# Second layer's first 1x1 convolution as seven block products, with the sums of h kept in the residual buffer's place

## Chip, cores and metric

The kernel runs on one core of one Trainium2 chip. The metric is the device time of one execution in microseconds; three executions of the kernel before gave 2811.97 to 2815.28, median 2813.42.

## What is computed

Two bottleneck layers in float32, on 64 images of 1024 channels and 14 x 14 positions:

```python
# layer 0: three convolutions with batch norm and a residual
out = relu(bn(conv1x1(x, w1)))            # 1024 -> 256
out = relu(bn(conv3x3(out, w2)))          # 256 -> 256
h   = relu(x + softplus(s) * bn(conv1x1(out, w3)))   # 256 -> 1024
# layer 1: a deformable bottleneck with group norm
a   = relu(group_norm(conv1x1(h, w1b)))   # 1024 -> 256, the convolution that is changed
off, mask = conv3x3(a, w_off)             # 27 offset and mask channels
s   = bilinear_sample(a, offsets) * mask  # 9 taps
b   = relu(group_norm(einsum(s, w2b)))    # 9 x 256 -> 256
out = relu(h + group_norm(conv1x1(b, w3b)))   # 256 -> 1024
```

## The kernel before

Images go in 32 pairs of 392 columns (196 for each image). Layer 0 runs first, in three stages up to about 960 us of the span; batch norm needs all images. Layer 1 is a software pipeline over the pairs. One pass of it is called a **slot** here: slot t runs the sampling and the second convolution of pair t, the first convolution and the offsets of pair t+1, the third convolution of pair t-1, and fetches h of pair t+2. Slots 2 to 29 are written by `steady`, where the order of the instructions on TensorE, VectorE, ScalarE and GpSimd is the order in which the list `todo` is run. The other slots are written by `slot`, where that holds for TensorE alone and a scheduler orders the rest. Every engine, and SyncE's queue of transfers, works its instructions off in order.

`put` and `at` weave work into a list of matmul steps: a step at position k is emitted ahead of the k-th matmul step. `weave` mixes two lists evenly.

A slot goes in this order on TensorE:

1. `first_conv(t+1)`, 16 products of 392 columns (L1130): eight blocks of input channels for each of two blocks of output channels. Each product is two matmul instructions. ScalarE copies a finished bank to `a1` (L1138), VectorE takes its statistics (L1006).
2. `sampling(t, 0)` (L1455) woven with the first half of `third_conv(t-1)` (L1704). Sampling multiplies by S, the product of the row and column weights that `corners` forms on VectorE (L1435, three pieces).
3. The offset convolution (L1226) of pair t+1, which reads X, four combinations of the columns of `a1` that VectorE writes (L1202) after the norm and relu (ScalarE, L1161).
4. `sampling(t, 1)` woven with the rest of the third convolution. The offsets `off` (L1257) and the mask go to DRAM and come back spread over the partitions as `wt` (SyncE, L1284); L1273 takes the largest offset; L1296 adds the base positions.
5. `second_conv(t, 0)` and `second_conv(t, 1)` (L1567), 35 and 28 products of 196 columns. This convolution and the third are done in seven block products for eight: of a 2 x 2 by 2 x 2 block product with blocks a and b, seven products of sums of blocks. The two column blocks are the two images of the pair. VectorE forms the sums of the sampled values in place (L1523); the banks are emptied by additions: E is a copy of the first bank (ScalarE), V is the second bank plus E (VectorE), and GpSimd adds V to E and to the fourth part.

The third convolution does its seven products m = 0 to 6 for each of four blocks of output channels, in the order 0, 2, 1, 3. V is L1711, GpSimd's two additions are L1716, and the two outputs are L1720 and L1724. Its product 6 is added to the bank half that product 3 wrote, after V has read it:

```python
bank = q["bank", 1 if m == 6 else m // 2]
nc.tensor.matmul(bank[:, m % 2 if m < 6 else 1], a, b, start=(m < 6), ...)
```

The banks of the first and third convolution and of the transposes come from one pool of three.

A group norm is a chain on VectorE from L1016 to L1054, a power on GpSimd (L1055), and the scale and shift on VectorE (L1071, L1075, L1078). gn1 belongs to the first convolution, gn2 to the second, gn3 to the third.

h of pair t+2 is made in place: SyncE loads the third convolution of layer 0, ScalarE scales it (L1096), two transfers on GpSimd's queue add x (L1102), ScalarE applies relu (L1111). For pairs up to 3 the sum is made on VectorE with `Z0` as a buffer (L213). From slot 2 on `Z0` is unused, except in a second run of the layer, which only starts if an offset is larger than 2.

`output` adds h to the scaled third convolution (L1803), applies relu (L1805) and stores; `scaled` is the scaling on ScalarE (L1787).

Of the kernel before, what the change touches and what calls it, by code (L numbers as in the profile page):

```python
# [10 lines left out]
FP = mybir.dt.float32  # L11
AF = mybir.ActivationFunctionType
ALU = mybir.AluOpType
# [7 lines left out]
CB = 8  # L21
# [23 lines left out]
def kernel(  # L45
# [823 lines left out]
    make_identity(nc, ident)  # L869


    goff = const.tile([P, MB * T, 32], FP, tag="goff", name="goff")
# [21 lines left out]

    Sb = {n: const.tile([P, 512], FP, tag=f"Sb{n}", name=f"Sb{n}") for n in (1, 2, 4)}
    Sb[3] = a21

    c11, c12, c21, c22 = (w2b_sb[:, c, :, ts(o, P)] for o in range(2) for c in range(2))
    Sc = {n: const.tile([P, T, P], FP, tag=f"Sc{n}", name=f"Sc{n}") for n in (1, 2, 4)}
# [25 lines left out]

    def build_second_bottleneck(l1, path, run, early):
        groups, R, tapsets = path.groups, path.rows, path.tapsets
        QR = R * W
        starts = sorted({r0 for _, _, chunks in groups for r0 in chunks})

# [177 lines left out]
        def first_relu(p):  # L1108
            for b in range(0, CB, 2):
                y = Y[p % 4][:, ds(b, 2)]  # L1110
                nc.scalar.activation(y, y, AF.Relu)  # L1111

        def residual(p, b0=0, b1=CB):

            for b in range(b0, b1):

                tc.keep_in_program_order(end_of_first(p, Z0, b))
                relu_of_first(p, b)

        def first_conv(p, by_inputs=False):  # L1120
            q = pairs[p]

            def step(o, c):
                if o == c == 0:
                    q["a1"] = two.tile([P, MB, N2], FP, tag="a1", name=f"a1_{p}")
                    q["gn1"] = Norm(MB, 8, N1S, N1B, f"gn1_{p}")
                    q["pt"] = {}
                if c == 0:
                    q["pt"][o] = ps.tile([P, N2], FP, tag="ps", name=f"d1_{p}_{o}")
                nc.tensor.matmul(  # L1130
                    q["pt"][o],
                    w1b_sb[:, c, ts(o, P)],
                    q["y"][:, c, :],
                    start=(c == 0),
                    stop=(c == CB - 1),
                )
# [7 lines left out]
            return [lambda o=o, c=c: step(o, c) for o, c in order]  # L1144

        def norm_steps(norm):

# [98 lines left out]
        def offsets(p):  # L1246
            q = pairs[p]
            half = W // 2
            (even, odd), (m0, m3) = q["sums"], (q["po"][ts(m, 32)] for m in (1, 3))

            q["om"] = one.tile([32, N2], FP, tag="off", name=f"off_{p}")
            for h0, h1, _ in groups:
                dst = q["om"][:, cols(h0, h1)].rearrange("p (i q n) -> p i q n", i=2, n=2)
                for n, (a, b, op) in enumerate(((even, m0, ALU.add), (odd, m3, ALU.subtract))):
                    a = a.rearrange("p (i q) -> p i q", i=2)
                    a, b = (v[:, :, h0 * half : h1 * half] for v in (a, b))
                    nc.vector.tensor_tensor(dst[:, :, :, n], a, b, op)  # L1257
# [165 lines left out]
                    .to_broadcast([R, W, piece.stop - piece.start]),  # L1423
                )

        def corners(p, e):

            q = pairs[p]
            S, X = q["S"][e], q["X"][e]
            k0, k1 = tapsets[e]  # L1430
            q["S"][e] = {}
            for g, r0, piece in pieces(e):

                tc.keep_in_program_order(
                    nc.vector.tensor_tensor(S[:, piece], S[:, piece], X(piece), ALU.mult)  # L1435
                )
                q["S"][e][g, r0] = S[:, piece].rearrange("q (k i n) -> q k i n", k=k1 - k0, i=2)

        def sampling(p, e):

            q = pairs[p]
            k0, k1 = tapsets[e]
            kt = k1 - k0
            out = []

            def step(turn, g, h0, h1, chunks, c, i0, ni):
                if turn == 0:
                    q["sm"][e] = sample_buffer(e, f"sm_{p}_{e}").rearrange(
                        "p (c k i q) -> p c k i q", c=MB, i=2, q=HW
                    )  # L1450
                n = (h1 - h0) * W
                pt = ps_s.tile([P, ni, kt, n], FP, tag="ps_s", name=f"sp_{p}_{e}_{g}_{c}_{i0}")
                for i in range(ni):
                    for j, r0 in enumerate(chunks):
                        nc.tensor.matmul(  # L1455
                            pt[:, i],
                            q["aT"][:, i0 + i, c, starts.index(r0), :],
                            q["S"][e][g, r0][:, :, i0 + i, :],
                            start=(j == 0),
                            stop=(j == len(chunks) - 1),  # L1460
                        )
# [300 lines left out]
        def third_norm(p, both=True):  # L1762
            q = pairs[p]

            def end():
                q["gn3"][0].scale(tc.keep_in_program_order)
                for m in range(2 if both else 1):
# [9 lines left out]
        def scaled(p, m):  # L1777

            q = pairs[p]
            n = q["gn3"][0]  # L1780
            if m in q.setdefault("scaled", set()):
                return
            q["scaled"].add(m)
            for b in range(m, CB, 2):
# [67 lines left out]
        def weight_sums():  # L1852
            for n, a, b, op in (
# [5 lines left out]

                tc.keep_in_program_order(nc.vector.tensor_tensor(Sb[n], a, b, op))  # L1860

        def slot(t):


# [31 lines left out]
            if d1:  # L1896
                extra = list(zip((5, 5, 8, 12, 12, 13, 13, 14), norm2)) + [(10, w) for w in weights[:1]]
                extra = sorted(extra + [(6, s) for s in late], key=lambda v: v[0])
                todo = put(d1, [s for _, s in extra], [k for k, _ in extra])
# [58 lines left out]
        def steady(t):  # L1958
# [9 lines left out]
            def at(steps, *extra):  # L1968
# [21 lines left out]
            todo += at(  # L1990
                pd[0],
                ((1, 1, 1, 9), norm3),
                ((5, 20), [lambda e=e: first_sum(t, e) for e in range(2)]),
                ((6, 11, 16, 21), transposes(t + 1)),
                ((6, 13), [distances, end]),
            )
            todo += [lambda: list(spread_rows(t + 1, 0)), lambda: list(spread_columns(t + 1, 0))]
            todo += [lambda: list(spread_rows(t + 1, 1)), lambda: lend(t + 1)]
            todo += at(pd[1], ((0,), [lambda: first_relu(t + 2)]), ((16,), [lambda: output(t - 1, 0)]))
            todo.append(lambda: list(spread_columns(t + 1, 1)))  # L2000
            for step in todo:
                step()
# [200 lines left out]
```

## Time and profile before

| | |
|---|---|
| median of 3 runs | 2813.42 us (2811.97 to 2815.28) |
| the profiled execution's own time | 2814.66 us |
| span of its instructions | 2812.9 us |
| granted TensorE clock | 0.991 |
| busy: TensorE, VectorE, ScalarE, GpSimd | 2750.9, 2264.8, 1424.8, 1043.1 us |
| first convolution of layer 1, L1130 | 1024 instructions, 345.3 us |
| second convolution, L1567 | 2232 and 1674 instructions, 400.6 and 308.3 us |
| transfers | 424.20 MB, mean 151 GB/s |

PE is TensorE, PEld its weight loads, DVE VectorE, ACT ScalarE, POOL GpSimd, SP SyncE. A line of the timeline gives the start in us from the span's start, the duration, engine, line, operation, out<-in, shape, count, and in brackets the idle time of the engine just before and what ended it. A row with a count covers neighbours that were merged. An instruction that does not depend on the one before it on its engine starts a little before that one's end.

### The profile page before, as it was taken

The numbers are of one execution on the slowest core, as the hardware profiler recorded it, in microseconds if no ns is written. First come the engines' busy times: TensorE is split into PE (matmuls) and PEld (weight loads), VectorE is DVE, ScalarE is ACT, GpSimd is POOL, SyncE is SP. The second block draws the span as 40 slices with busy tenths as digits, with TensorE's granted clock in tenths as the row PEclk, the third lists the DMA queues.
The fourth block names the chain that finished last, engine by engine and source line by source line (L and its number), as shares of the span: only waits on it lengthen the run. The fifth ranks groups of instructions, "written<-read, shape, count | busy, mean of one in ns | idle before, by whom it ended". The sixth has DMA issues, their size and how long they took to land.

```text
span 2812.9 us, 39583 instructions
## 1 busy us (share of the span) xinstructions
PE 2750.9 (98%) x12930; PEld 2016.8 (72%) x12930; DVE 2264.8 (81%) x4676; ACT 1424.8 (51%) x2835; POOL 1043.1 (37%) x1125
## 2 busy tenths in 40 slices
PE   9999899998999999999999999999999999999996
PEld 5555555554555567887888788878887888888874
DVE  7877899998888878878777878788778787777776
ACT  0000221212555546666666676667666766676653
POOL 4630366663666312323332333233323332332221
PEclk9999999999999999999999999999999999999998
DMA  8656000003555444667576657665767576657641
GB/s 236 191 172 175 23 1 0 1 1 132 215 197 219 177 137 167 165 169 196 161 168 175 194 154 173 176 190 153 173 173 200 146 175 177 193 147 175 183 125 48
DMA packets 350317, 424.20 MB, mean 151 GB/s; under 512 B 27892, under 2 KB 292500, under 8 KB 349844
## 3 DMA queue, kind: packets, MB, share of 16 engines
q1 hardware_dynamic: 291860, 376.61, 41.3%
q0 software_dynamic: 58240, 44.96, 11.3%
q8 instruction: 104, 1.70, 0.3%
q14 instruction: 113, 0.93, 0.1%
HBM read 296.49 MB, written 116.76 MB: 147 GB/s over the span
## 4 chain that ended last, share of the span: by engine, by line
PE 59%; DVE 2%; issue 1%; DMA 1%; SPq 0%; ACT 0%; POOL 0%; DVEq 0%; ACTq 0%; POOLq 0%
PE pd L1567 21%; PE sp L1455 12%; PE d L1130 11%; PE d L1704 10%; PE om L1226 2%; PE tr L1333 1%; DMA X<-wd 1%; PE pd L1486 1%; DMA wt<-dm 0%; DVE st L1006 0%; SPq L1374 0%; DVE sm L1523 0%; DMA wd<-wt 0%; SPq L1418 0%; DVE z L1818 0%
## 5 line engine op out<-in xcount | busy, mean ns | idle before, releaser
L1455 PE MATMUL sp<-S,aT 126*128 126x420 f32 (+3 forms) x1536 | 487.0, 415 | 8.0 <-DVE S L1435 5.5
L1567 PE MATMUL pd<-sm,w2b_sb 128*128 128x196 f32 x2232 | 400.6, 329 | 0.0
L1463 ACT COPY sm<-sp 128x336 f32<-128x336 f32 (+3 forms) x640 | 282.8, 447 | 187.8 <-PE sp L1455 167.7
L1567 PEld LDWEIGHTS pd<-sm,w2b_sb 128*128 128x128 f32 x2232 | 371.2, 190 | 0.0
L1523 DVE TENSOR_TENSOR sm<-sm 128x980 f32<-128x980 f32 (+2 forms) x257 | 268.5, 1055 | 120.9 <-PE pd L1567 116.8
L530 PE MATMUL c<-v,u_sb 128*128 128x392 f32 x1024 | 342.6, 497 | 11.0 <-DVE bn1sh L167 8.2
L1130 PE MATMUL d<-h,w1b_sb 128*128 128x392 f32 x1024 | 345.3, 495 | 2.7 <-ACT h L224 2.7
L1567 PE MATMUL pd<-sm,Sc 128*128 128x196 f32 x1674 | 308.3, 329 | 0.6 <-DVE sm L1523 0.6
L530 PEld LDWEIGHTS c<-v,u_sb 128*128 128x128 f32 x1024 | 194.6, 191 | 158.9 <-issue 11.3
L1130 PEld LDWEIGHTS d<-h,w1b_sb 128*128 128x128 f32 x1024 | 194.0, 191 | 139.5 <-ACT h L224 6.4
L1567 PEld LDWEIGHTS pd<-sm,Sc 128*128 128x128 f32 x1674 | 278.7, 190 | 1.1 <-ACT wt L1297 0.9
L1455 PEld LDWEIGHTS sp<-S,aT 126*128 126x128 f32 x1536 | 258.5, 191 | 20.7 <-issue 9.0
L1787 ACT ACTIVATE z<-z,gn_0sh,gn_0sc 128x196 f32<-128x196 f32 x496 | 225.1, 536 | 18.0 <-DVE gn_0sh L1078 18.0
L1598 POOL TENSOR_TENSOR E<-V,E 128x196 f32<-128x196 f32 x31 | 18.5, 597 | 516.8 <-DVE V L1597 516.8
L516 DVE TENSOR_TENSOR v<-t 128x392 f32<-128x392 f32 x256 | 192.9, 811 | 0.0
L1704 PE MATMUL d<-h,w3b_sb 128*128 128x196 f32 x744 | 174.0, 329 | 0.8 <-ACT h L1619 0.8
L1704 PEld LDWEIGHTS d<-h,w3b_sb 128*128 128x128 f32 x744 | 133.6, 189 | 51.6 <-issue 19.1
L1435 DVE TENSOR_TENSOR S<-S,X 126x840 f32<-126x840 f32 (+1 forms) x192 | 159.5, 880 | 11.7 <-DMA X<-wd 11.3
L1805 ACT ACTIVATE z<-z 128x784 f32<-128x784 f32 x124 | 105.8, 856 | 105.1 <-DVE z L1803 102.7
L385 PE MATMUL c<-xc,w1a_sb 128*128 128x392 f32 x384 | 149.1, 497 | 5.3 <-DMA xc<-in_x_dram 5.3
L1096 ACT ACTIVATE h<-h,bn3sh,bn3sc 128x392 f32<-128x392 f32 x224 | 149.9, 705 | 0.0
L504 POOL TENSOR_TENSOR t<-wpad 128x784 f32<-128x784 f32 x62 | 95.2, 1536 | 127.2 <-DVE v L516 127.2
(693 smaller groups left out, 5044.3 us busy)
## 6 DMA issues: line engine op xcount, KB each, us to landing
xc<-in_x_dram SPq DMA_DIRECT2D x128, 392.0 KB
h<-o SPq DMA_DIRECT2D x64, 784.0 KB
h<-h SPq DMA_DIRECT2D x64, 784.0 KB
out_dram<-z SPq DMA_DIRECT2D x124, 392.0 KB
h<-in_x_dram POOLq DMA_DIRECT2D x56, 784.0 KB, 12.5
X<-wd SPq DMA_DIRECT2D x64, 413.4 KB
S<-wd SPq DMA_DIRECT2D x64, 413.4 KB
S<-wd SPq DMA_DIRECT2D x64, 330.8 KB
```

Of the source, the lines that this page charges most:

```text
L385: nc.tensor.matmul(acc[m], a, b, start=(j == 0), stop=(j == HB - 1))
L516: nc.vector.tensor_tensor(v[:, u].rearrange("p (i y x) -> p i y x", y=7, x=7), cols[c][:, :, i : i + 13 : 2, :], cols[c][:, :, j : j + 13 ...
L530: nc.tensor.matmul(m[u], u_sb[:, c, u, k % 4, ts(o, P)], vts[k][c][:, u], start=(c == 0), stop=(c == MB - 1),)
L1096: nc.scalar.activation(y, y, AF.Identity, bias=bn3.sh[:, b : b + 1], scale=bn3.sc[:, b : b + 1])
L1130: nc.tensor.matmul(q["pt"][o], w1b_sb[:, c, ts(o, P)], q["y"][:, c, :], start=(c == 0), stop=(c == CB - 1),)
L1435: nc.vector.tensor_tensor(S[:, piece], S[:, piece], X(piece), ALU.mult)
L1455: nc.tensor.matmul(pt[:, i], q["aT"][:, i0 + i, c, starts.index(r0), :], q["S"][e][g, r0][:, :, i0 + i, :], start=(j == 0), stop=(j == len ...
L1463: nc.scalar.copy(dst, pt.rearrange("p i k n -> p k i n"))
L1523: return nc.vector.tensor_tensor(dst, a, b, ALU.subtract)
L1567: nc.tensor.matmul(bank[:, m % 2], a[:, k], b[:, k - k0],  start=(k == 0 and m in (5, 0, 2, 6)), stop=(k == T - 1), skip_group_check=True,)
L1704: nc.tensor.matmul(bank[:, m % 2 if m < 6 else 1], a, b, start=(m < 6), stop=True, skip_group_check=True)
L1787: nc.scalar.activation(z[:, ts(i, HW)], z[:, ts(i, HW)], AF.Identity, bias=n.sh[:, b, i : i + 1], scale=n.sc[:, b, i : i + 1],)
```

## The change

From pair 3 on, the first 1x1 convolution of layer 1 is done in seven block products. The 1024 input channels are two blocks of four times 128, the 256 output channels two blocks, the columns the two images. A product is 4 matmul steps of 196 columns, so 28 steps take the place of 16 of 392.

- The sums of the weights are formed once, in slot 1, on VectorE (`first_weight_sums`): three in a new tile `Sa`, one in place in `w1b_sb`. The offset weights' staging tile `goff` now lies in `Sa`.
- The sums of h, T1[1] to T1[4], are formed for each pair on VectorE by `first_sums` in `Z0`: for pair t+2 in slot t, three ahead of the second half of the second convolution and one at its position 22 of 28.
- The banks are emptied as in the third convolution: E by ScalarE, V and the two outputs by VectorE, two additions by GpSimd. `a1` is complete only at the end; before, its first half was copied after half of the products.
- `off` has no tile of its own any more and lies in `wt`'s.
- Positions: `corners(t, 0)` is cut into its three pieces, at 19 and 24 of the 28 steps and behind them; gn2's scale, relus and sums are at 17 to 19; relu of h moves from the start of the second half of the second convolution to position 24 of the first half, ahead of four of the eight scalings of the third convolution's blocks 0, 2, 4, 6.

```diff
+    Sa = const.tile([P, 3, HB, P], FP, tag="Sa", name="Sa")
+    goff = Sa.rearrange("p n k o -> p (n k o)")[:, : MB * T * 32].rearrange("p (n o) -> p n o", o=32)
...
+    e11, e12, e21, e22 = (w1b_sb[:, ts(c, HB), ts(o, P)] for o in range(2) for c in range(2))
+    Se = {1: Sa[:, 0], 2: Sa[:, 1], 3: e21, 4: Sa[:, 2]}
...
+        def first_sums(p, *ns):
+            q, room = pairs[p], Z0.rearrange("p b n -> p (b n)")
+            T1 = q.setdefault("T1", {})
+            y = q["y"]
+            (b11, b12), (b21, b22) = ([y[:, ts(c, HB), ts(i, HW)] for i in range(2)] for c in range(2))
+            for n in ns:
+                T1[n] = room[:, ts(n - 1, HB * HW)].rearrange("p (b q) -> p b q", b=HB)
+                a, b = ((b12, b11), (b22, T1.get(1)), (b22, b12), (b21, T1.get(2)))[n - 1]
+                tc.keep_in_program_order(nc.vector.tensor_tensor(T1[n], a, b, ALU.subtract))
...
         def first_conv(p, by_inputs=False):
+            if early and p >= 3:
+                return first_conv_of_seven(p)
...
+        def first_conv_of_seven(p):
...
+                a, b = (
+                    (e11, b11),
+                    (Se[1], T1[1]),
+                    (Se[2], T1[2]),
+                    (Se[3], T1[3]),
+                    (e12, b21),
+                    (Se[4], b22),
+                    (e22, T1[4]),
+                )[m]
+                if k == 0 and m in (0, 2, 4):
+                    q["bank", m // 2] = ps.tile([P, 2, HW], FP, tag="ps", name=f"d1_{p}_{m}")
+                bank = q["bank", 1 if m == 6 else m // 2]
+                nc.tensor.matmul(
+                    bank[:, m % 2 if m < 6 else 1],
+                    a[:, k],
+                    b[:, k],
...
+                if m == 1:
+                    q["E"] = one.tile([P, 2, HW], FP, tag="E", name=f"E1_{p}")
+                    nc.scalar.copy(q["E"], bank)
+                elif m == 3:
+                    E = q["E"]
+                    V = q["V"] = one.tile([P, 2, HW], FP, tag="V", name=f"V1_{p}")
+                    nc.vector.tensor_tensor(V, bank, E, ALU.add)
+                    nc.gpsimd.tensor_tensor(E[:, 1], V[:, 0], E[:, 1], ALU.add)
+                    nc.gpsimd.tensor_tensor(a1[:, 1, HW:], V[:, 0], V[:, 1], ALU.add)
+                elif m == 5:
+                    nc.vector.tensor_tensor(
+                        a1[:, 0].rearrange("p (i n) -> p i n", i=2), bank, q["E"], ALU.add
+                    )
+                    q["gn1"].stats(0, a1[:, 0])
+                elif m == 6:
+                    nc.vector.tensor_tensor(a1[:, 1, :HW], bank[:, 1], q["V"][:, 0], ALU.add)
+                    q["gn1"].stats(1, a1[:, 1])
+            return [lambda m=m, k=k: step(m, k) for m in range(7) for k in range(HB)]
...
-            q["om"] = one.tile([32, N2], FP, tag="off", name=f"off_{p}")
+            q["om"] = one.tile([KY, 2, N2], FP, tag="wt", name=f"off_{p}")[:32, 0, :]
...
+            if early and t == 1:
+                todo.append(first_weight_sums)
...
+            if early and t == 1:
+                todo.append(lambda: first_sums(3, 1, 2, 3, 4))
...
         def steady(t):
...
                 ((0,), [lambda: scaled(t - 2, 1)]),
-                ((1, 1, 7, 9, 9, 10, 10, 10), norm2),
-                ((6,), [lambda: output(t - 2, 1)]),
-                ((7,), [lambda: load(t + 2, False)]),
-                ((10,), [lambda: corners(t, 0)]),
+                ((2, 2, 17, 18, 18, 18, 18, 19), norm2),
+                ((12,), [lambda: output(t - 2, 1)]),
+                ((13,), [lambda: load(t + 2, False)]),
+                ((19, 24), [lambda n=n: corners(t, 0, n) for n in range(2)]),
             )
+            todo += [lambda: corners(t, 0, 2)]
             todo += at(weave(sp[0], d3[:half]), ((4, 4, 8, 14, 16, 18, 21), norm1))
...
                 pd[0],
                 ((1, 1, 1, 9), norm3),
+                ((24, 25), [lambda: first_relu(t + 2), lambda: scaled(t - 1, 0, 4, CB)]),
...
-            todo += at(pd[1], ((0,), [lambda: first_relu(t + 2)]), ((16,), [lambda: output(t - 1, 0)]))
+            todo += at(
+                pd[1],
+                ((0, 22), [lambda: first_sums(t + 2, 1, 2, 3), lambda: first_sums(t + 2, 4)]),
+                ((16,), [lambda: output(t - 1, 0)]),
+            )
```

More of the change, by code (lines that the diff above doesn't have):

```diff
@@ L869 @@
     make_identity(nc, ident)
-    goff = const.tile([P, MB * T, 32], FP, tag="goff", name="goff")
+    Sa = const.tile([P, 3, HB, P], FP, tag="Sa", name="Sa")
+    goff = Sa.rearrange("p n k o -> p (n k o)")[:, : MB * T * 32].rearrange("p (n o) -> p n o", o=32)
     woff_sb = const.tile([P, 4, MB * 3, 32], FP, tag="woff", name="woff_sb")
@@ L927, in build_second_bottleneck @@
         groups, R, tapsets = path.groups, path.rows, path.tapsets
+        if not early:
+            nc.sync.dma_start(e21, w1b[: HB * P, ds(P, P)].rearrange("(b p) o -> p b o", p=P))
         QR = R * W
@@ L1144, in first_conv, with step @@
             return [lambda o=o, c=c: step(o, c) for o, c in order]
+        def first_conv_of_seven(p):
+            q = pairs[p]
+            def step(m, k):
+                if m == k == 0:
+                    q["a1"] = two.tile([P, MB, N2], FP, tag="a1", name=f"a1_{p}")
+                    q["gn1"] = Norm(MB, 8, N1S, N1B, f"gn1_{p}")
+                y, T1, a1 = q["y"], q["T1"], q["a1"]
+                (b11, b12), (b21, b22) = (
+                    [y[:, ts(c, HB), ts(i, HW)] for i in range(2)] for c in range(2)
+                )
[15 more added lines that the diff above has]
+                    b[:, k],
+                    start=(k == 0 and m < 6),
+                    stop=(k == HB - 1),
+                    skip_group_check=True,
+                )
+                if k < HB - 1:
+                    return
+                if m == 1:
[10 more added lines that the diff above has]
+                        a1[:, 0].rearrange("p (i n) -> p i n", i=2), bank, q["E"], ALU.add
+                    )
+                    q["gn1"].stats(0, a1[:, 0])
[3 more added lines that the diff above has]
+            return [lambda m=m, k=k: step(m, k) for m in range(7) for k in range(HB)]
@@ L1424, in spread_columns, with corners @@
                 )
-        def corners(p, e):
+        def corners(p, e, *ns):
             q = pairs[p]
@@ L1430, in corners @@
             k0, k1 = tapsets[e]
-            q["S"][e] = {}
-            for g, r0, piece in pieces(e):
+            done = q.setdefault(("corner", e), {})
+            for n, (g, r0, piece) in enumerate(pieces(e)):
+                if ns and n not in ns:
+                    continue
                 tc.keep_in_program_order(
@@ L1436, in corners @@
                 )
-                q["S"][e][g, r0] = S[:, piece].rearrange("q (k i n) -> q k i n", k=k1 - k0, i=2)
+                done[g, r0] = S[:, piece].rearrange("q (k i n) -> q k i n", k=k1 - k0, i=2)
         def sampling(p, e):
@@ L1457, in step @@
                             q["aT"][:, i0 + i, c, starts.index(r0), :],
-                            q["S"][e][g, r0][:, :, i0 + i, :],
+                            q["corner", e][g, r0][:, :, i0 + i, :],
                             start=(j == 0),
@@ L1766, in end @@
                 q["gn3"][0].scale(tc.keep_in_program_order)
-                for m in range(2 if both else 1):
+                if not both:
+                    scaled(p, 0, 0, 4)
+                    return
+                for m in range(2):
                     scaled(p, m)
@@ L1775, in third_norm, with scaled @@
             ]
-        def scaled(p, m):
+        def scaled(p, m, b0=0, b1=CB):
             q = pairs[p]
             n = q["gn3"][0]
[L1781 to L1784, printed above, removed]
+            done = q.setdefault("scaled", set())
+            for b in range(b0 + m, b1, 2):
+                if b in done:
+                    continue
+                done.add(b)
                 z = z_of(p, b)
@@ L1860, in weight_sums, with first_weight_sums @@
                 tc.keep_in_program_order(nc.vector.tensor_tensor(Sb[n], a, b, op))
+        def first_weight_sums():
+            for n, a, b, op in (
+                (1, e21, e22, ALU.add),
+                (2, Se[1], e11, ALU.subtract),
+                (3, e11, e21, ALU.subtract),
+                (4, e12, Se[2], ALU.subtract),
+            ):
+                tc.keep_in_program_order(nc.vector.tensor_tensor(Se[n], a, b, op))
         def slot(t):
@@ L1898, in slot @@
                 extra = sorted(extra + [(6, s) for s in late], key=lambda v: v[0])
-                todo = put(d1, [s for _, s in extra], [k for k, _ in extra])
+                todo = put(d1, [s for _, s in extra], [k * len(d1) // 16 for k, _ in extra])
                 todo += put(weave(sp[0], d3[:half]), norm1, (4, 4, 8, 14, 16, 18, 21))
@@ L1998, in steady @@
             todo += [lambda: list(spread_rows(t + 1, 1)), lambda: lend(t + 1)]
-            todo += at(pd[1], ((0,), [lambda: first_relu(t + 2)]), ((16,), [lambda: output(t - 1, 0)]))
+            todo += at(
+                pd[1],
+                ((0, 22), [lambda: first_sums(t + 2, 1, 2, 3), lambda: first_sums(t + 2, 4)]),
+                ((16,), [lambda: output(t - 1, 0)]),
+            )
             todo.append(lambda: list(spread_columns(t + 1, 1)))
```

## Prediction

> **What bounds the kernel now.** The page comes first: TensorE is busy 98% of the span, every other engine 81% or less. The chain that ended last goes on TensorE through the whole second layer, and its products L1130 open a slot every 56.0 us (at 1546.35 and at 1602.35, 10.53 us each).
>
> ```profile
> PE 2750.9 (98%) x12930; PEld 2016.8 (72%) x12930; DVE 2264.8 (81%) x4676; ACT 1424.8 (51%) x2835; POOL 1043.1 (37%) x1125
> ```
>
> So a slot is TensorE work without a gap, and less of it should be a shorter slot. But the average hides the stage that is changed. I cut one slot (t = 11) at its stages: first the products L1130, last the second half of the second convolution.
>
> ```profile
> core 0: us, PE busy (x) PEld busy (x) DVE busy (x) ACT busy (x) POOL busy (x), PEclk, DMA share, GB/s
> 1602.19:1612.72 10.53, 10.53 (x34) 6.08 (x33) 9.10 (x21) 5.92 (x12) 4.36 (x6) 1.00 0.82 262
> ...
> 1648.90:1658.19 9.29, 9.29 (x58) 9.29 (x58) 5.63 (x7) 5.90 (x10) 0.41 (x1) 1.00 0.58 196
> ```
>
> In the first stage VectorE is busy 9.10 of 10.53 us, hardly less than TensorE, and the change shortens TensorE's share and lengthens VectorE's. Next, VectorE's queue through that stage and just behind it, from the timeline (start, duration, idle before):
>
> ```profile
> 1606.62 1.85 DVE L1803 TENSOR_TENSOR z<-z,h 128x784 f32<-128x784 f32 x2
> ...
> 1610.26 3.14 DVE L1435 TENSOR_TENSOR S<-S,X 126x840 f32<-126x840 f32 x3
> ...
> 1614.05 0.31 DVE L1016 STREAM_TRANSPOSE gn_12R<-st 128x128 f32<-128x128 f32 x1
> ...
> 1616.03 0.17 DVE L1054 TENSOR_SCALAR gn_12B<-gn_12B 128x4 f32<-128x4 f32 x1
> 1616.44 0.57 DVE L1711 TENSOR_TENSOR V<-d,E 128x392 f32<-128x392 f32 x1 [0.25 <-PE d L1704]
> 1617.32 0.55 DVE L1071 SCALAR_TENSOR_TENSOR gn_12sc<-gn_12B,vec 128x4 f32<-128x4 f32 x1 [0.30 <-POOL gn_12B L1055]
> 1617.90 0.53 DVE L1075 SCALAR_TENSOR_TENSOR gn_12sh<-gn_12B,gn_12sc 128x4 f32<-128x4 f32 x1
> ...
> 1618.64 0.57 DVE L1720 TENSOR_TENSOR z<-d,E 128x392 f32<-128x392 f32 x1
> 1619.12 0.35 DVE L1724 TENSOR_TENSOR z<-d,V 128x196 f32<-128x196 f32 x1
> ```
>
> The idle times in brackets are all the room there is. TensorE meets this queue twice in the third convolution: its seventh product of the first column block may overwrite a bank only when V (L1711) has read it, and the third product of the second block needs the bank that L1724 empties.
>
> ```profile
> 1602.19 10.70 PE L1130 MATMUL d<-h,w1b_sb 128*128 128x392 f32 x32
> ...
> 1618.02 0.50 PE L1704 MATMUL d<-T,w3b_sb 128*128 128x196 f32 x2
> ...
> 1620.21 0.50 PE L1704 MATMUL d<-T,Sb 128*128 128x196 f32 x2
> ```
>
> V ends at 1617.01, 1.01 us before its product at 1618.02; L1724 ends at 1619.47, 0.74 us before 1620.21. These two margins decide the case.
>
> **What is removed.** 32 matmul instructions of 392 columns take 10.53 us, 0.329 each. 28 products are 56 instructions of 196 columns; L1567 dispatches ten such in 1.66 us, 0.166 each. 56 x 0.166 = 9.29, so 1.24 us less per slot: 54.76 if nothing else moves. The two ScalarE copies L1138 (0.48 each) become one. A rule speaks against this: the Trainium skill, "TensorE: Matmul & The Clock Gate", section "Back-to-back issue gap", gives streams of weight load and matmul 81 ns each at 128 columns and 131 at 512, far from proportional. An estimate by that page (90 ns at 196 columns, 115 at 392) would make the stage 10.53 x 56/32 x 0.78 = 14.4 us, 3.8 us more per slot. The rows here are proportional, with 2232 weight loads hidden, and I go by them.
>
> **What is added to VectorE.** Evictions: one add of 392 from a bank (0.57, as L1711), another (0.57, as L1720), one of 196 (0.35, as L1724): 1.49 us, in the first stage. Sums of h: four subtractions of 784 at 0.97 (row L1523), 3.6 to 3.9 us, in the last stage. A slot's VectorE time goes from 44.2 to about 49.6 of 54.76: it fits on average, so the place decides. GpSimd gets two adds of 196 (0.60 each, as L1598).
>
> **The sums' place.** VectorE idles before the first sm subtraction and before V of the second convolution:
>
> ```profile
> 1650.43 0.98 DVE L1523 TENSOR_TENSOR sm<-sm 128x784 f32<-128x784 f32 x1 [3.22 <-PE pd L1567]
> ...
> 1657.13 0.57 DVE L1597 TENSOR_TENSOR V<-pd,E 128x392 f32<-128x392 f32 x1 [1.30 <-PE pd L1567]
> ```
>
> The relu of h is moved up, from 1648.03 to behind four of the eight z scalings (L1787, 3.64 us for eight) and three aT copies, so to about 1646.3, which is when the accumulating transfer of x lands in a median slot (13.6 us after its second issue at 1632.7). The first sum then starts near 1647.9, the third ends near 1651.3, and the sm subtraction behind them runs 1651.2 to 1652.2; TensorE reads it at 1654.2, so it is covered by 2 us, and the next two are back on time. The fourth sum takes 0.89 of the 1.30 us before V. So the sums are free by 0.4 us. ScalarE waits there in order; if x lands later, its z scalings and the sums slide, and beyond 0.4 us V slides with them. Landings spread over 1.5 us: I take 1 us over the whole run, bounds 0 and 6.
>
> **The evictions' place, step by step in the slot shown.** A row that does not depend on the one before starts 0.08 us before that ends.
> - L1803 ends at 1608.47 as before. New V: 1608.39 to 1608.96. GpSimd's new adds follow: 1609.04 to 1609.64 and to 1610.19.
> - The scale of gn2 (three rows of 0.16) came at 1608.49. Now its first row goes through and the other two meet the GpSimd adds. The rows L1071 and L1075 above show what that is: 0.55 and 0.53 for 0.16, each ending with one of the two adds L1716 (1617.25 and 1617.81, 0.60 each). So it is done at 1610.21, for 1609.04.
> - First corner product (1.01): to 1611.14. New add: 1611.06 to 1611.63, its bank complete since 1610.3. Statistics: to 1612.23. Second corner product: held by GpSimd's T sums to 1612.60, done 1612.93. New add of 196: to 1613.20, statistics to 1613.81, third corner product held to 1613.95, done 1614.88.
> - Norm chain L1016 to L1054, 2.15 us: 1614.92 to 1617.07; before, it ended at 1616.20, so 0.87 later.
> - V: 1616.99 to 1617.56. GpSimd's power (1.01) ends 1618.15; scale behind the L1716 adds; L1720; L1724 ends 1620.34, again 0.87 later.
>
> **TensorE.** Its seventh product, 1.24 earlier, is due at 1616.78. What a release costs is seen where VectorE held TensorE up in slot t = 18: the subtraction ends 2036.33, the product starts 0.14 later.
>
> ```profile
> 2035.15 1.17 DVE L1523 TENSOR_TENSOR sm<-sm 128x980 f32<-128x980 f32 x1
> ...
> 2036.47 0.57 PE L1567 MATMUL pd<-sm,Sc 128*128 128x196 f32 x2 [0.61 <-DVE sm L1523]
> ```
>
> So it starts at 1617.70, 0.92 late. The third product of the next block is then due at 1619.89 and starts at 1620.48, 0.59 late. Gain 1.24, stalls 1.51: the slot is 56.27 us, 0.27 longer. Behind this point VectorE idles 2.00 us before X (L1202) and is back in step, so nothing more adds up.
>
> The trace does not show how the new rows meet GpSimd. Lower end: none is held; scale 0.77, corners 0.39 and 0.14 less, slot 54.97. Upper end: one more corner at 1.43, the longest that it took in this slot, slot 56.67. I take 56.27, because the held scale has its exact likeness in L1071 and L1075.
>
> **Small terms.** The offsets now lie in wt's buffer, so the wt transfers, issued at 1632.20, wait for the omax reduction (L1273, ends 1632.77) and go 0.6 later; on SyncE's queue only mk stands behind them before the next long pause. The wt addition already waited for them in four slots, up to 1.42 us, of which about 0.7 is covered: 1.4 us over the run. In slots 1 and 2: four weight sums of about 0.55 among the sm subtractions, a stall of 0.5; the sums for pair 3 stand behind the second convolution's statistics, first one done near 1102.3, where the second product is due at 1099.3: 3.1; norm chain later by 0.6 more. Together 4.2, bounds 1 and 8. The moved offset of ScalarE's other z scalings: they end at 1651.1, L1803 needs them at 1654: free. The loads of h (L204) and the two stores ahead of them are emitted later, but wait for L1803, which ends at 1608.47 in either order, and keep their place in SyncE's queue: free. The reload of a weight block stands in the second run, which does not start. Slot 30: gain against stall, 0, bounds -1.2 and +1.
>
> **Sum.** 27 x 0.27 = 7.3, and 4.2, 1.4, 1.0: 13.9 us on the profiled execution's 2814.66 (span 2812.90 and 1.76 around it), 2828.6. That execution lies 1.24 above the median of the runs, so 2827.
>
> **Rivals.** (a) VectorE keeps up: the scale slips in ahead of GpSimd, or corners are not held. For it: 0.77 us of my 2.1 us delay is one meeting of short rows. Slots 54.76 to 55.5 give 27 x -1.24 to -0.5, with 6.6 of small terms: 2786 to 2806. This is the case that ends faster; it decides from a norm chain that ends before 1616.3. (b) The stalls just eat the gain: slot 55.55 to 55.96, between -5.6 and +5.6 us. (c) x lands too late each time: V slides by 0.4 us more, 2838; for it, the queue of transfers is full there (share 1.00 in the stage before); against, the median slot has 0.4 us left.
>
> **Chances and range.** About 0.2% (5.6 us) is what a measurement of this kernel tells from no change. Forecast slower by more than that, with (c) in it, 0.58 (0.48 and 0.10); no change (b) 0.14; faster (a) 0.28. The range goes from all rows unheld (27 x -1.03 + 6.6 = -21, 2792) to the upper end (27 x 0.67 + 10 = +28, 2842); the forecast's own range is 2819 to 2842.
>
> **What would show it.** Right: TensorE idles before the third convolution's product with T and w3b and before the next block's third, released by V and z, about 0.9 and 0.6 us a slot; L1071 of gn2 and its followers near 0.5 us; slots of about 56.3. Wrong: slots under 55.5 with no such idle time, or stalls elsewhere, first of all at the new d products (sums late) or at the offset convolution.

## The result, and the profile after

The changed kernel takes 2819.96 us (median of 20 runs, 2816.64 to 2824.08), the kernel before 2812.78 (20 runs on the same chip, 2811.20 to 2816.31): a ratio of 1.0024, interval 1.0018 to 1.0031. It is slower, as forecast, but by 7.2 us and not by 13.6.

The span of the profiled execution is 2819.7 us, 6.8 more than before. The first line of the page, and then one window for the first stage and one for a whole slot (columns as before: start and end, length, busy time of PE, PEld, DVE, ACT, POOL, clock):

```profile
PE 2741.1 (97%) x13626; PEld 2108.7 (75%) x13626; DVE 2406.1 (85%) x4883; ACT 1415.2 (50%) x2806; POOL 1048.2 (37%) x1183
```

```profile
1664.31:1673.60 9.29, 9.29 (x58) 9.29 (x58) 8.58 (x20) 5.56 (x11) 3.75 (x6) 1.00 0.77 263
1608.41:1664.31 55.90, 55.58 (x343) 49.62 (x343) 49.03 (x105) 36.59 (x75) 17.75 (x24) 1.00 0.67 178
```

The stage is down from 10.53 to 9.29 us, to the hundredth what the rows of before gave. The prediction also gave an estimate of 14.4 us, worked out from the Trainium skill, "TensorE: Matmul & The Clock Gate", section "Back-to-back issue gap". The trace does not agree with it: 9.29 us, and 196 columns cost half of 392. Yet the slot is 55.90 us, where 54.76 would be the full gain. TensorE's waits, over the 26 slots 3 to 28, name who took it (engine, tile, line, releaser, us in total, times, longest):

```profile
PE d L1780 <- DVE V L1787: 6.6, 26, 0.3
PE sp L1531 <- ACT sm L1539: 2.2, 7, 0.6
PE pd L1643 <- DVE sm L1599: 0.6, 1, 0.6
```

Before, the same view of the same slots has only the last kind, once, 0.6 us. The times shown are the idle parts alone, and the view leaves out the smallest. What a wait costs is read better from the starts of TensorE's rows against those of before, both counted from the first product of the slot (the rows are below): 1.24 us ahead at the start of the third convolution; 0.45 ahead after the product that waits for V, with the short wait for ScalarE's `sm` in front of it; 0.14 ahead after the third product of the next block; 0.10 ahead at the end. So a slot loses 0.79, 0.31 and 0.04 of its 1.24 us.

Over the run: pair 3's first product comes 3.0 us later than before (1.0 of it from layer 0, which ends anywhere in 2.8 us in the profiles of the study, 2.0 from slots 0 and 1); slot 2 is 3.5 us longer; the 26 slots 3 to 28 take 0.2 us less in all (median 55.94 for 56.00, some wide ones up to 56.72); slot 29 is 1.5 longer; the tail is 1.0 shorter. That is the 6.8.

VectorE's queue in slot t = 12, whose start is 62.12 us later than that of the slot shown of before (timeline: start, duration, engine, line, operation). This slot is one of the wide ones, 56.72 us, but for another reason and at its end; the rows shown are as in a steady slot.

```profile
1670.52 0.56 DVE L1206 TENSOR_TENSOR V<-d,E 128x392 f32<-128x392 f32 x1
1671.00 0.15 DVE L1078 SCALAR_TENSOR_TENSOR gn_11sc<-gn_11B,vec 128x4 f32<-128x4 f32 x1
1671.18 0.59 DVE L1082 SCALAR_TENSOR_TENSOR gn_11sh<-gn_11B,gn_11sc 128x4 f32<-128x4 f32 x1
1671.81 0.52 DVE L1085 TENSOR_TENSOR gn_11sh<-gn_11sh,vec 128x4 f32<-128x4 f32 x1
1672.26 1.02 DVE L1511 TENSOR_TENSOR S<-S,X 126x840 f32<-126x840 f32 x1
...
1675.89 1.06 DVE L1511 TENSOR_TENSOR S<-S,X 126x840 f32<-126x840 f32 x1
...
1678.92 0.56 DVE L1787 TENSOR_TENSOR V<-d,E 128x392 f32<-128x392 f32 x1
...
1681.46 0.57 DVE L1796 TENSOR_TENSOR z<-d,E 128x392 f32<-128x392 f32 x1
1681.95 0.35 DVE L1800 TENSOR_TENSOR z<-d,V 128x196 f32<-128x196 f32 x1
```

```profile
1679.63 0.57 PE L1780 MATMUL d<-T,w3b_sb 128*128 128x196 f32 x2 [0.25 <-DVE V L1787]
1680.03 0.49 PE L1780 MATMUL d<-h,w3b_sb 128*128 128x196 f32 x2
...
1682.09 0.60 PE L1780 MATMUL d<-T,Sb 128*128 128x196 f32 x2
1682.52 0.87 PE L1531 MATMUL sp<-S,aT 126*128 126x420 f32 x2
```

Before, the rows behind the same two products were these (the slot starts at 1602.19 there and at 1664.31 here):

```profile
1618.36 0.49 PE L1704 MATMUL d<-h,w3b_sb 128*128 128x196 f32 x2
...
1620.54 0.87 PE L1455 MATMUL sp<-S,aT 126*128 126x420 f32 x2
```

In VectorE's rows, see the first row of the scale slip through (0.15) and the next two held by GpSimd's two additions (0.59, 0.52), V ending 0.15 before the product that waits for it, and the third product of the next block starting at 1682.09 while L1800 is still at work until 1682.30.

### The profile page after: what moved, and what is told of

Read it like the earlier page. It is cut to its first block, busy times and chain, and to the rows that moved or that the text cites. A ratio compares the mean times of both kernels' runs of the same rounds, so it can differ in the third digit from the quotient of the medians.

```text
span 2819.7 us, 41384 instructions
## 1 busy us (share of the span) xinstructions
PE 2741.1 (97%) x13626; PEld 2108.7 (75%) x13626; DVE 2406.1 (85%) x4883; ACT 1415.2 (50%) x2806; POOL 1048.2 (37%) x1183
## 4 chain that ended last, share of the span: by engine, by line
PE 55%; DVE 4%; DMA 3%; issue 2%; ACT 1%; SPq 1%; POOL 0%; DVEq 0%; ACTq 0%; POOLq 0%
PE pd L1643 20%; PE sp L1531 12%; PE d L1780 10%; PE d L1190 9%; PE om L1300 2%; DMA X<-wd 1%; PE tr L1407 1%; DVE V L1787 1%; DMA wt<-dm 1%; PE pd L1562 1%; DVE sm L1599 0%; DVE st L1013 0%; ACT sm L1539 0%; DMA S<-wd 0%; SPq L1448 0%
## 5 line engine op out<-in xcount | busy, mean ns | idle before, releaser
L1190 PE MATMUL d<-h,w1b_sb 128*128 128x196 f32 x928 | 168.2, 329 | 0.0
L1511 DVE TENSOR_TENSOR S<-S,X 126x840 f32<-126x840 f32 (+1 forms) x192 | 150.8, 813 | 10.7 <-DMA X<-wd 9.7
L1190 PEld LDWEIGHTS d<-h,w1b_sb 128*128 128x128 f32 x928 | 155.9, 190 | 0.2 <-DVE V L1206 0.2
```

The source lines that it names most:

```text
L1190: nc.tensor.matmul(bank[:, m % 2 if m < 6 else 1], a[:, k], b[:, k], start=(k == 0 and m < 6), stop=(k == HB - 1), skip_group_check=True,)
```

## The experiments

The theory that was tested (A): VectorE works through its queue without a gap from the first stage on, gn2's scale is held in it by GpSimd, and the rows behind it reach TensorE late. The rivals: the sums of h, the landings of x, or the transfers of `wt` set the slot. Ratios are to the kernel before on the same chip; for the changed kernel the ratio is 1.0024.

**Scale of gn2 ahead of the new V.**

```diff
-                ((2, 2, 17, 18, 18, 18, 18, 19), norm2),
+                ((2, 2, 15, 18, 18, 18, 18, 19), norm2),
```

> One position changed: the scale of gn2 (three rows of VectorE) is emitted at position 15 of the 28 steps instead of 17, so ahead of the new V, and meets no GpSimd addition. Theory A (VectorE's queue in the first stage is what eats the 1.24 us): its rows fall from 0.16, 0.59, 0.52 us to about 0.16 each, everything behind them comes 0.5 to 0.8 us earlier, the relus of ScalarE too, so TensorE's waits of 0.28 (sp), 0.51 (V) and 0.29 us (z) shrink by 0.5 to 0.8 together. Slots of 55.1 to 55.4 us, whole 2800 to 2806. Rival B (the sums of h, or the landings of x, set the slot): VectorE's gain is lost at the next wait in the last stages, slots stay within 0.1 us of 55.91 and the time at 2818 to 2821.

Measured: 2808.58 us, ratio 0.9979 (0.9970 to 0.9988), faster than both kernels, but above the 2800 to 2806 expected. Steady slots are 55.51 us, 0.40 less, where 0.5 to 0.8 was expected. The three rows are free; what was lost again is seen one row later, on VectorE and on GpSimd:

```profile
1609.88 0.16 DVE L1078 SCALAR_TENSOR_TENSOR gn_10sc<-gn_10B,vec 128x4 f32<-128x4 f32 x1
1610.07 0.16 DVE L1082 SCALAR_TENSOR_TENSOR gn_10sh<-gn_10B,gn_10sc 128x4 f32<-128x4 f32 x1
1610.27 0.16 DVE L1085 TENSOR_TENSOR gn_10sh<-gn_10sh,vec 128x4 f32<-128x4 f32 x1
...
1610.83 1.02 DVE L1511 TENSOR_TENSOR S<-S,X 126x840 f32<-126x840 f32 x1
1612.36 0.57 DVE L1210 TENSOR_TENSOR a<-d,E 128x392 f32<-128x392 f32 x1 [0.50 <-POOL E L1207]
```

```profile
1611.00 1.32 POOL L1207 TENSOR_TENSOR E<-V,E 128x196 f32<-128x196 f32 x1 [1.15 <-DVE V L1206]
```

Now the corner is there first, and GpSimd's addition takes 1.32 us for 0.60; the next addition on VectorE waits 0.50 for it. Theory A holds in kind; the collision is moved, not removed. By the starts of TensorE's rows, the first stall is down to 0.40 us, and the second is what it was, 0.30.

**The first output addition of the third convolution ahead of gn1's scale**, alone and with the edit above.

```diff
-            todo += at(weave(sp[0], d3[:half]), ((4, 4, 8, 14, 16, 18, 21), norm1))
+            todo += at(weave(sp[0], d3[:half]), ((4, 4, 10, 14, 16, 18, 21), norm1))
```

> One position changed: the scale and shift of gn1 are emitted at position 10 of the woven list instead of 8, so behind V and the first output addition of the third convolution, which then does not stand behind their wait for GpSimd's power. Theory A: the wait of 0.51 us for V stays, the 0.29 us before the third product of the next block go, slots of about 55.6 us, whole 2811 to 2813; X and the offset convolution have the room for a later gn1. Rival B (that wait is by the bank that the other addition empties, as the prediction had it): no change for the third product, slots 55.9, 2819 to 2821; if gn1 comes too late for X, a new wait before the offset convolution, up to 0.6 us a slot, 2836.

> Both positions changed together. Theory A: nearly all of the three waits goes (1.08 us a slot), slots 54.8 to 55.1 us, 27 slots x -0.8 to -1.1 on 2820: 2790 to 2798, faster than the kernel before (2812.8). Rival B (the slot is set elsewhere): 2815 or more.

Measured: 2851.0 (1.0136, 1.0120 to 1.0151) and 2839.79 (1.0092, 1.0078 to 1.0106). Both expectations missed, but the first kernel answers the question about the bank. Its TensorE and VectorE:

```profile
1635.86 0.50 PE L1780 MATMUL d<-T,Sb 128*128 128x196 f32 x2
```

```profile
1634.67 0.57 DVE L1796 TENSOR_TENSOR z<-d,E 128x392 f32<-128x392 f32 x1 [1.22 <-POOL E L1792]
...
1635.62 0.35 DVE L1800 TENSOR_TENSOR z<-d,V 128x196 f32<-128x196 f32 x1
```

The third product waits no more and starts at 1635.86, before L1800 ends (1635.97): the bank it needs is the one that L1796 empties. The time was lost at a wait that the forecast had as a small term. VectorE's waits over slots 3 to 28 of the same kernel, and one such place in its timeline:

```profile
DVE wt L1370 <- DMA wt<-dm: 29.8, 18, 2.1
```

```profile
1658.57 0.97 DVE L1370 TENSOR_TENSOR wt<-wt,base_sb 126x784 f32<-126x784 f32 x1 [1.64 <-DMA wt<-dm]
```

The transfers of `wt` are issued only 0.3 us later in the slot than in the changed kernel. But they land so late that in most slots the addition waits 1.1 to 2.1 us, and the `sm` subtraction behind the addition holds TensorE up (18.2 us in 21 slots). In slots 3 to 29 of these two kernels, the addition waits over 1 us in 44 of the 47 slots where the first `wt` transfer was issued 0.40 us or more after the second transfer of x, and in none of the 7 where it was 0.32 or less. In slots 3 to 28 of the changed kernel the distance is 0.15 to 0.24, and the addition waits over 1 us in one slot, slot 12; in slot 29 it is 0.63, and the wait is 2.12. Before the change `wt` was issued 0.47 ahead in a median slot.

**The sums of h left out.** The products read h where they should read T1.

```diff
-                T1[n] = room[:, ts(n - 1, HB * HW)].rearrange("p (b q) -> p b q", b=HB)
-                a, b = ((b12, b11), (b22, T1.get(1)), (b22, b12), (b21, T1.get(2)))[n - 1]
-                tc.keep_in_program_order(nc.vector.tensor_tensor(T1[n], a, b, ALU.subtract))
+                T1[n] = (b12, b22, b12, b21)[n - 1]
```

> Leaves out the four sums of h: the products read h itself where they should read T1, all else stays. Theory A (the sums are hidden in steady slots and cost only where slot 2 starts): slots 3 to 28 stay at 55.85 to 55.95 us; slot 2 loses the wait of 2.3 us before its second product; slots with a late landing gain a few tenths; whole 2815 to 2818. Rival B (the sums are what eats the gain): slots of 55.0 to 55.4 us, whole 2796 to 2808.

Measured: 2814.41, ratio 1.0000 (0.9991 to 1.0009), 0.6 under the time expected. Steady slots are 55.89 to 55.91, as with the sums; slot 2 takes 56.48 for 59.70, slot 29 55.89 for 57.51, and most of the slots around 56.1 are gone. The sums are hidden in a steady slot; they cost where the pipeline starts and where a transfer lands late.

**The two additions of the output's second half left out** (theory A's cost by itself: 1.94 us less of VectorE ahead of the new V).

```diff
+                if not (m == 1 and 1 <= p < NP - 3):
                     tc.keep_in_program_order(
                         nc.vector.tensor_tensor(part, part, q["y"][:, 2 * b + m : 2 * b + m + 3 : 2], ALU.add)
```

> Leaves out the two additions of h in the second half of the output (pairs 1 to 28), 0.97 us each on VectorE in the first stage, ahead of the new V; nothing else changes. Theory A (VectorE's queue through the first stage eats the gain): V of the third convolution comes 0.7 to 1.0 us earlier and with it the relus of ScalarE; slots of 54.9 to 55.3 us, whole 2794 to 2803. Rival B (another engine or transfer sets the slot): 2817 to 2821, with the idle time moved to a later stage.

Measured: 2799.93, ratio 0.9953 (0.9940 to 0.9967), slots 55.29, both as theory A has it. In the view of waits, TensorE's wait for V is left once in slots 3 to 28, where the changed kernel has it 26 times:

```profile
PE d L1780 <- DVE V L1787: 0.2, 1, 0.2
```

Of the 1.94 us only 0.6 came back, because VectorE now idles ahead of the new V, until TensorE has filled the bank:

```profile
1606.56 0.57 DVE L1206 TENSOR_TENSOR V<-d,E 128x392 f32<-128x392 f32 x1 [1.05 <-PE d L1190]
```

The 0.53 us that a slot still lacks to 54.76 is lost behind this row: by the starts of TensorE's rows, 0.18 at the product that needs V, 0.30 at the third product of the next block, as before the edit, and the rest later.

**The largest-offset reduction moved up**, to right behind the offsets, so that the shared buffer is free earlier: with both edits, alone, and with the scale ahead.

```diff
                     nc.vector.tensor_tensor(dst[:, :, :, n], a, b, op)
+            nc.vector.tensor_reduce(
+                omax[:, p : p + 1], q["om"], mybir.AxisListType.X, ALU.max, apply_absolute_value=True
+            )
```

> Both positions changed, and the reduction that takes the largest offset stands right behind the offsets on VectorE, ahead of two statistics and two additions, so that the buffer shared by the offsets and wt comes free about 1.4 us earlier. Theory A2 (with z first, the wt transfers are issued 0.4 us behind the second transfer of x instead of 0.15, get behind its packets, and the wt addition waits 1.2 to 2.1 us): they are issued at or ahead of the second x again, the wait goes, slots of 54.8 to 55.2 us, whole 2786 to 2798. Rival B2 (the gn1 scale is simply too late for X and the offsets, whatever the transfers do): the wt addition still waits over 1 us, slots of 56.3 to 57, whole 2825 to 2840.

> The changed kernel with only that reduction moved ahead. Theory A2: steady slots stay at 55.9, since their time is set in the first stage; the slots with a late wt (57.51, 56.72, and those of 56.1 to 56.5 beside them) come back towards 55.9; whole 2814 to 2818. Rival (the wide slots come from x, not from wt): 2819 to 2821.

> The scale of gn2 ahead, gn1 as in the changed kernel, and the reduction moved ahead. Theory A2: slots of 55.5 as without the move, the few wide ones (56.78, 56.14, 56.00) lose most of their surplus: whole 2805 to 2808. Rival: no change from the kernel with the scale ahead, 2808 to 2810.

Measured: 2823.65 (1.0034, 1.0021 to 1.0046), 2833.16 (1.0068, 1.0054 to 1.0082), 2820.98 (1.0024, 1.0014 to 1.0035). All three times missed, and half of the theory held: in the first, the addition of `wt` never waits, where with both edits alone it waited over 1 us in most slots. But steady slots are 56.18, 56.49 and 56.08, all alike. Two statistics and the reduction now stand in front of the addition that empties a bank for the block after (TensorE's waits over slots 3 to 29 of the first of the three; lines are 5 lower here, so L1791 is the changed kernel's L1796):

```profile
PE d L1775 <- DVE z L1791: 14.2, 27, 0.6
```

**The sharing undone.** From slot 2 on the offsets lie in S's buffer, which is free at that time.

```diff
-            q["om"] = one.tile([KY, 2, N2], FP, tag="wt", name=f"off_{p}")[:32, 0, :]
+            if early and 3 <= p < NP - 1:
+                q["om"] = one.tile([QR, wide * KT[0]], FP, tag="S0", name=f"off_{p}")[:32, :N2]
+            else:
+                q["om"] = one.tile([KY, 2, N2], FP, tag="wt", name=f"off_{p}")[:32, 0, :]
```

> The changed kernel with the sharing undone in slots 2 to 29: the offsets lie in the free buffer of S, not in wt's. Theory A2 (the sharing makes wt's transfers wait for the largest-offset reduction, so that they are issued behind the second transfer of x and now and then land late): wt is issued 0.5 us earlier, the slots of 57.51 and 56.72 fall to about 56, steady slots stay at 55.9; whole 2816 to 2818. Rival (late landings have another cause): 2819 to 2821.

Measured: 2816.61, ratio 1.0013 (1.0004 to 1.0022), as expected. Slot 29 falls to 55.94, the slot of 56.72 to 55.87, and the steady ones stay at 55.88. So the small term of the `wt` transfers was there: slots 3 to 29 of the profile are 3.2 us shorter in all. The intervals of this ratio and of 1.0024 touch, so the whole time alone would not show it.

**Combined with the scale ahead, and weight sums in slot 0.**

```diff
-            if early and t == 1:
+            if early and t == 0:
                 todo.append(first_weight_sums)
```

> Scale of gn2 ahead, offsets in S's buffer, and the weight sums formed in slot 0, where VectorE idles 3.8 us, instead of slot 1. Expected: slots of 55.5, without the wide ones of 56.8 and 56.1 (-2 to -3 us in all), slot 2's start 0.5 to 1.5 us earlier: whole 2803 to 2806, faster than before (2813 to 2814). If the weight sums cost nothing in slot 1 and wt is not the cause of the wide slots: 2808 to 2810.

Measured: 2806.46, ratio 0.9966 (0.9954 to 0.9978), 6.9 us under the kernel before and 0.5 over the time expected. It has the lowest ratio of the complete kernels, but its interval overlaps that of the scale ahead alone (0.9970 to 0.9988). Steady slots are 55.50. Two parts of the expectation missed. Slot 29 is still wide, 57.27 in the profiled execution, with `wt` issued 0.82 us behind the second x. And from the first product of layer 1 to that of pair 3 it takes 131.95 us, where the kernel with the scale ahead alone took 131.09; another kernel with the same move, the last one below, took 130.88. That spread is as large as what the move could gain, so its worth is not shown.

**Statistics behind the output addition** (they were ahead of it), once with the scale and the reduction ahead, once with the scale, the first output addition, the offsets in S's buffer and the weight sums in slot 0.

```diff
-                    stats(before[j])
                 elif m == 5:
                     nc.vector.tensor_tensor(
                         z[0].rearrange("p (i n) -> p i n", i=2), bank, q["E"], ALU.add
                     )
+                    stats(before[j])
```

> Scale of gn2 ahead and reduction ahead, and the third convolution's statistics of the block before moved behind the first output addition instead of ahead of it. Theory (with the reduction ahead, two statistics and the reduction stand in front of the addition that empties the bank, and TensorE waits 0.65 us there in every slot): that wait goes, slots back to 55.4 to 55.5, and wt on time: whole 2803 to 2807. Rival (the reduction itself, or the earlier wt transfers, cost the 0.6 us): slots stay at 56.1, 2819 to 2822.

> Scale of gn2 ahead, scale of gn1 behind the first output addition, offsets in S's buffer, statistics behind the output addition, weight sums in slot 0. If what made the kernels with z first slow was the late wt alone (over 1 us of waiting in most slots): no wait there, slots of 55.2 to 55.5, whole 2796 to 2806. If the later gn1 costs by itself (X and the offset convolution): slots of 55.7 to 56.0, whole 2810 to 2818.

Measured: 2833.82 (1.0071, 1.0057 to 1.0085) and 2830.24 (1.0057, 1.0043 to 1.0071), steady slots 56.41 and 56.38. Both missed. The wait for z that they were to remove is gone, in the second kernel `wt` is on time but for two slots, and a new wait stands in every one of slots 3 to 28, at the second half of the sampling (second kernel; L1514 is `corners`, L1511 of the changed kernel):

```profile
1636.65 0.80 PE L1534 MATMUL sp<-S,aT 126*128 126x336 f32 x2 [0.89 <-DVE S L1514]
```

In the changed kernel V, the statistics (1.06 us) and X follow each other without a gap. In the second kernel VectorE idles 0.30 us in front of X, X takes 1.89 for 1.45 us, and the statistics then stand between the addition and the corners, which TensorE needs next. In the first kernel the view names ScalarE's scaling of h as the releaser of that wait (17.3 us in 26 slots), so for it this reading is not shown.

## Where the prediction was right, and the step that failed

**What bounds the slot: right.** VectorE's queue from the first stage on eats most of the gain. Shortening it (scale ahead, additions left out) gives back 0.40 and 0.6 of the 1.14 us that were lost; the rest is lost behind the new V.

**The evictions' place: right to 0.2 us.** Shifted by 62.12, against the forecast: new V 1608.40 to 1608.96 (1608.39 to 1608.96); scale done at 1610.21 (1610.21); first corner 1611.16 (1611.14); third corner 1614.83 (1614.88); norm chain 1616.89 (1617.07); V 1617.36 (1617.56). The rows that were held were the ones named, but for the third corner: it was put at held, and took 1.06 us where a free one takes 1.02.

**The first stall: 0.92 forecast, 0.79 measured**, the wait for ScalarE's `sm` in it. V came 0.2 earlier than the sum had it, most of it because the norm chain starts 0.08 before the third corner ends and not 0.04 after. The wait for ScalarE was not in the prediction; the wait for V, which ends later, takes it in.

**The second stall is the step that failed: 0.59 forecast, 0.31 measured.** The prediction said that the third product of the next block "needs the bank that L1724 empties". It needs the one that L1720 (L1796 after) empties, 0.26 earlier by the prediction's own queue (1620.08 for 1620.34): in all of slots 3 to 28 it starts 0.05 us after L1796 ends and 0.2 before L1800 ends. With that end and the 0.14 of a release the stall is 0.33, and the slot of the prediction's own sum 56.01 instead of 56.27. Both parts together, with the 0.04 lost later, make the median slot 55.94 us and not 56.27: 0.33 us a slot, some 9 us over 27 slots. So the term of +7.3 was in truth -1.6 for the median slot (55.94 for 56.00). That is more than the gap between the 13.9 of the sum and the 6.8 of the span; the small terms, below, took some of it back. The trace of before could not tell the two additions apart, since both had long ended (1619.21 and 1619.47) when the product started at 1620.21; the choice of one should have stood in the bounds, as an end of the range.

**Small terms: right in kind.** Start: 4.2 forecast, 5.5 measured (2.0 in slots 0 and 1, where other profiles of the study have 0.3 to 1.5, and 3.5 in slot 2), within the bounds of 1 to 8. Of slot 2, 3.2 are the sums for pair 3, as the run without sums shows, and the wait itself is in the timeline of the changed kernel:

```profile
1104.73 1.59 PE L1190 MATMUL d<-h,Sa 128*128 128x196 f32 x8 [2.32 <-DVE h L1130]
```

`wt` and late x: 1.4 and 1.0 forecast; what slots 3 to 29 take above the median slot grew by 2.9 in the profiled execution. Slot 30 was put at 0; with the tail it gave 1.0 back. The 1.0 of layer 0 has nothing to do with the change. Together: -1.6, 5.5, 2.9, -1.0 and 1.0 make the 6.8. The sums in steady slots were forecast free by 0.4 us; V behind them idles 0.36:

```profile
1661.93 0.96 DVE L1130 TENSOR_TENSOR h<-h,h 128x784 f32<-128x784 f32 x1
1663.25 0.56 DVE L1673 TENSOR_TENSOR V<-pd,E 128x392 f32<-128x392 f32 x1 [0.36 <-PE pd L1643]
```

**The rivals.** (a) was not the case: the norm chain ends at 1616.89, behind its point of decision, 1616.3. The steady slots are those of (b), 55.55 to 55.96. So the direction came out as forecast, but not by the term that was to carry it: 7.3 of the 13.9 us were to come from longer slots, and the slots came out no longer. The whole is slower only because the start and the late transfers add what a steady slot does not; that much of the hit is luck.

## What to carry to other kernels

Where a stall hangs on which of two releases frees a buffer, and both are early in the old trace, work the sum with each; a wrong choice of 0.26 us times 27 slots was 7.0 us, as much as the whole effect. A saving on the bound engine is worth only what the next engine's in-order queue lets through, so list the rows that stand in front of each release and ask what held them. And when a row is moved out of the way of one consumer, look whom it then stands in front of: of five moves here that did what they were meant to (the scale, the output addition, the reduction, the offsets' buffer, the statistics), three cost more at the next place.

## What the runs showed of the hardware

The hold between VectorE and GpSimd goes both ways. In the changed kernel VectorE's scale rows took 0.59 and 0.52 for 0.16 beside GpSimd's additions; with the scale ahead, the addition took 1.32 for 0.60 beside a corner that had started 0.17 earlier. The Trainium skill, "SBUF — State Buffer", section "SBUF: two separate sides", says that of a VectorE instruction with two SBUF inputs and a GpSimd one that reads SBUF, whichever starts first has the shared ports for its whole instruction. The trace agrees in both directions, with the durations above; the prediction had used only one.

A transfer issued 0.3 us later made its reader wait 1.1 to 2.1 us in most slots, when that put it 0.4 us behind a transfer of 784 KB on another queue. The kernels in which it was issued earlier again (the reduction moved up, or the buffer not shared) had no such wait in the steady slots. The distance is not all: slot 12 of the changed kernel has a wait of 1.37 us at a distance of 0.17. Why the step is so sharp was not measured.

The other long slot of the changed kernel, slot 17 (56.52 us), stays where the reduction is moved up or the buffer is not shared (56.4 to 56.8 us). In it one row of VectorE, the statistics of `a`, starts after 0.46 us of idle time, which it has in no other of the slots 3 to 28, and V comes 0.6 us later than in a steady slot. The profile names a GpSimd instruction as what ended that idle time, but the statistics do not read what it writes; the cause stays open.
